# Relative attention with 64-row score products: each half of the matrix array works on its own eight sequences

## The chip, the cores and the metric

The kernel runs on one core of a Trainium2 chip. The metric is the device time of one execution in microseconds (us), as the median of the runs. The profile of one execution gives, for each engine, when every instruction began and how long it took: PE is the matrix engine's products and PEld its loads of stationary operands, DVE the vector engine, ACT the scalar engine, POOL the general engine, SP the engine that issues most transfers.

## The reference

Sixteen sequences of 512 rows by 128 features go through a layer norm, and then through two branches that are added to the input: an attention with relative positions (16 heads of 8 features), and a network of three layers with weights of plus and minus one. Cut to what matters:

```
xn = layernorm(x)                                   # x: 16 x 512 x 128
q, k, v = heads of layernorm2(xn) @ Wq, Wk, Wv (+ biases)     # 16 heads of 8
p = heads of pe @ Wp                                # 512 positions
content = einsum('bihd,bjhd->bhij', q + u_bias, k)
pos     = relative_shift(einsum('bihd,jhd->bhij', q + v_bias, p))
attn    = softmax((content + pos) * scale, axis=-1)
head    = einsum('bhij,bjhd->bihd', attn, v)
out     = x + head @ Wo + bo + ffn(xn)
```

`relative_shift` pads each row of `pos` with a zero and reads the result back in rows of 512, so that query row i and key j meet the position at a distance that depends on j - i; above the diagonal the values are those of query row i + 1.

## The kernel before, in words

**Setup.** Norms, the three layers, and the projections of queries, keys and values come first. Queries and keys are kept as high and low halves of 16 bits, so that a product over 8 features becomes one over 4 parts x 8 = 32 rows. They are stored to scratch in HBM (`qu_scr`, `qv_scr`, `k_scr`, `p_scr`, `pd_scr`) and loaded again head by head. The stores of `qv_scr` are `quads_stored` (lines 595 to 602), eight transfers a call, issued by SP. Two of its four calls stand between the end of the projections and the first scores.

**Units.** Attention works in units: one head and 16 query rows (4 rows in each of 4 blocks of 128), all 16 sequences, all 512 keys. There are 16 heads x 32 = 512 units. The scores of a unit lie with the keys on the partitions, in two PSUM banks of 512 values: bank 0 has key blocks 0 and 1, bank 1 has key blocks 2 and 3, each with all 16 sequences. There are three pairs of such banks (`s_t`, line 791), so that a unit's banks come free when the exponentials of the unit three back have been taken.

**Scores** (`scores`, line 799, called for each half). All products have 128 rows. The stationary operand of a content product (line 811) holds the keys of four sequences, 32 rows each; the moving operand holds the queries of the four sequences beside zeros, so that one product of 64 columns gives the scores of four sequences. A half unit has 8 content products of 64 columns, 4 position products off the diagonal (line 827, two of 128 and two of 64 columns) and 2 on it (line 840, 64 columns).

**Maxima.** DVE takes the maximum over the first bank's two key blocks (`max_first`, L854), then folds in the two blocks of the second bank (`max_second`, L859, twice). PE turns the result with two transposes (L864), and DVE takes the maximum over the keys (L868), negated. PE adds it to the scores with four products of 256 columns (L873, two for each bank), and ACT takes the exponential of each bank (L883), written for the pair of 16 units into a large tile in SBUF, of which there are two.

**Values.** `weighted` (L904) multiplies one sequence group's exponentials with the values and a column of ones: four products with 9 stationary columns each, placed at columns 0, 32, 64 and 96 of the array, in 32-bit precision, which the profile shows as two records each. A pair of 16 units has 16 such blocks; two are issued in each cycle, one behind the other.

**Order.** The order of PE, DVE and ACT is written out by hand: `STEPS` (line 41) lists one cycle, which is two units, and each engine works through its own steps in that order. There are 256 full cycles. A step `A0` belongs to the first unit of the cycle, `G1-` to the second unit of the cycle before. A and B are the two halves of the scores, F, G and H the maxima, T the transposes, N the maximum over keys, X and Y the subtraction and exponential of each half, V two blocks of values. SP issues the loads for the next heads and query rows in between (`load_queries`, `load_head`, two of them at each A step). When a pair is done, its sums go to HBM by POOL's queue, are divided there and come back; the output projection is spread over later cycles (`first_output`, `rest`, `direct`). `direct` (L1066) has products with a 9-row stationary operand at rows 0, 32, 64 and 96.

Of the kernel before, what the change touches and what calls it, by code (L numbers as in the profile page):

```python
# [40 lines left out]
STEPS = "N0- A0 B0 G1- H1- X0- F0 Y0- T1- N1- V G0 X1- A1 Y1- H0 T0 B1 F1"  # L41
# [17 lines left out]
def attention_order():  # L59

    cycles = UP // 2
    last = H * NU // 2
    for c in range(last + 1 + cycles):  # L70
        for step in STEPS.split():
            if step == "V":
                if c > cycles:
                    yield "V", *divmod(c - 1 - cycles, cycles)
                elif c < cycles:
                    yield "W", c
                continue
            late = step.endswith("-")
            if late <= c < last + late:
                yield step[0], 2 * (c - late) + int(step[1])  # L80
# [3 lines left out]
def rel_attention_and_binary_ffn(  # L84
# [53 lines left out]
    qv_scr = scr("qv_scr", [4, DH * H, 5, NL, NC, UL, B], F16)  # L138
# [23 lines left out]
    win = [cst(f"win_{n}", [P, 2, WIN], F16) for n in range(2)]  # L162
    win_d = [cst(f"win_d_{n}", [P, 2, WIND], F16) for n in range(2)]
    q_t = [cst(f"q_{n}", [P, 16, S], F16) for n in range(2)]
    qc_t = [t[:, :4].rearrange("p g (n i m) -> p g n i m", n=2, m=2) for t in q_t]
    qp_t = [t[:, 4:12].rearrange("p (s r) (a u b) -> p s r a u b", s=2, a=NC, u=UL) for t in q_t]
    qd_t = [t[:, 12:].rearrange("p (t r) (a u b) -> p t r a u b", t=2, a=NC, u=UL) for t in q_t]
# [15 lines left out]
    def load_head(h, m):  # L183

        src = p_scr.rearrange("t (d h) s j -> (t d) h s j", h=H)[:, h]
        src_d = pd_scr.rearrange("t (d h) s n j -> (t d) h s n j", h=H)[:, h]

        def load(n):
            rows_n = slice(32 * n, 32 * n + 32)
            nc.sync.dma_start(  # L190
                k_t[m][rows_n], k_scr.rearrange("t (d h) b j -> (t d) h b j", h=H)[:, h, n::4, :]
            )
            nc.sync.dma_start(win[m][rows_n], src[:, :, 3 - n : 3 - n + WIN])
            r, side = n // 2, n % 2
            nc.sync.dma_start(win_d[m][rows_n], src_d[:, side, :, 1 - r : 1 - r + WIND])

        return [lambda n=n: load(n) for n in range(4)]
# [4 lines left out]
    def load_queries(h, l):  # L202

        m = l % 2
        qv = qv_scr.rearrange("t (d h) r l a u b -> (t d) h r l (a u b)", h=H)[:, h, :, l]
        qu = qu_scr.rearrange("t (d h) b n i m -> (t d) h b n (i m)", h=H)[:, h]

        def load(n):
            rows_n = slice(32 * n, 32 * n + 32)
            nc.sync.dma_start(  # L210
                qc_t[m][rows_n, :, n // 2].rearrange("p g i m -> p g (i m)"),
                qu[:, n // 2 :: 2, n % 2, 2 * l * P : 2 * (l + 1) * P],
            )
            nc.sync.dma_start(
                qp_t[m][rows_n, :, n].rearrange("p s a u b -> p s (a u b)"), qv[:, n : n + 2]
            )
            r, side = n // 2, n % 2
            nc.sync.dma_start(
                qd_t[m][rows_n, :, r].rearrange("p t a u b -> p t (a u b)"),
                qv[:, r + side : r + side + 3 : 2],  # L220
            )

        return [lambda n=n: load(n) for n in range(4)]


    with ExitStack() as pre:
# [29 lines left out]
        def load_x(b):  # L256
# [12 lines left out]
        after = [next_place(places, [NL * NC, UL, B]) for _ in range(2)]  # L269
        p_half = [  # L270
            t.rearrange("p x u b -> p (x u b)")[:, : PAD + S + PAD] for t in after
        ]
        qv_all = [next_place(places, [4, NQ, B]) for n in range(2)]
# [11 lines left out]
        for t in after:  # L285
            nc.vector.memset(t.rearrange("p x u b -> p (x u b)").bitcast(F32)[:, : PAD + S // 2], 0.0)
# [220 lines left out]
        def clear_queries(b):  # L507

            nc.gpsimd.memset(q_t[b % 2][:, 2 * (b // 2) : 2 * (b // 2) + 2].bitcast(F32), 0.0)
# [29 lines left out]
        def project_q(b):  # L539
# [10 lines left out]
            for m in range(2):  # L550
# [5 lines left out]
                q_banks.rearrange("p n (q r) -> p r q n", r=4), 1, *[q[:, :, :, b : b + 2] for q in qv_all]  # L556
# [28 lines left out]
        def next_quads():  # L585

            for n in range(2):
                first = qv_all[n][:, 0].rearrange("p (x u) b -> p x u b", u=UL)
                end = NL * NC - NC
                nc.scalar.copy(after[n][:, :, : UL - 1], first[:, :, 1:])  # L590
                nc.scalar.copy(after[n][:, :end, UL - 1], first[:, NC:, 0])
                nc.scalar.copy(after[n][:, end : end + NC - 1, UL - 1], first[:, 1:NC, 0])
                nc.vector.memset(after[n][:, end + NC - 1, UL - 1], 0.0)

        def quads_stored(l):
            for n in range(2):
                src = qv_all[n].rearrange("p r (l q) b -> p r l (q b)", l=NL)[:, :, l]
                last = after[n].rearrange("p (l a) u b -> p l (a u b)", l=NL)[:, l]
                for part in Q_PARTS[n]:
                    dst = qv_scr[part].rearrange("f r l a u b -> f r l (a u b)")[:, :, l]  # L600
                    nc.sync.dma_start(dst[:, :4], src)
                    nc.sync.dma_start(dst[:, 4], last)
# [185 lines left out]
    with ExitStack() as att:  # L788
        ps = att.enter_context(tc.tile_pool(name="ps", bufs=1, space=bass.MemoryType.PSUM))

        s_t = [
            [ps.tile([P, 2, NC, 4, B], F32, tag=f"s_{n}_{m}", name=f"s_{n}_{m}") for m in range(2)]
            for n in range(3)
        ]
        t_t = ps.tile([P, 4, 2, P], BF16, tag="t", name="t_t")
        t_bank = t_t.rearrange("p n f i -> p (n f i)").bitcast(F32).rearrange("p (g i) -> p g i", g=2)
        manual = ExitStack()
        manual.enter_context(tc.manual_schedule(engines=ORDERED))
        def scores(n, half, st):

            side_m, u = st["m"], st["u"]
            sp = st["ps"][half]
            blocks = sp.rearrange("p c a r b -> p (c a) r b")
            kt = k_t[side_m]
            m = (u // UL) % 2
            qc = qc_t[m].rearrange("p g n (a i) m -> p g n a i m", a=NC)
            qp, qd = qp_t[m], qd_t[m]
            ul = u % UL
            for c in (2 * half, 2 * half + 1):
                for g in range(4):  # L810
                    nc.tensor.matmul(  # L811
                        sp[:, c % 2, :, :, 4 * g : 4 * g + 4].rearrange("p a r (n m) -> p n (a r) m", m=2),
                        lhsT=kt[:, g, c * P : (c + 1) * P],
                        rhs=qc[:, g, :, :, 4 * ul : 4 * ul + 4].rearrange("p n a r m -> p n a (r m)"),
                        start=(c % 2 == 0 and g == 0),
                        stop=False,
                        skip_group_check=True,
                    )

            for side, off, dist in ((0, LO_OFF, range(-1, -NC, -1)), (1, UP_OFF, range(1, NC))):  # L820
                for d in dist:
                    cs = [c for c in (2 * half, 2 * half + 1) if 0 <= c - d < NC]
                    if not cs:
                        continue
                    x0 = (cs[0] % 2) * NC + cs[0] - d
                    y0 = off + d * P - 4 * u
                    nc.tensor.matmul(  # L827
                        blocks[:, x0 : x0 + (NC + 1) * (len(cs) - 1) + 1 : NC + 1],
                        lhsT=win[side_m][:, side, y0 : y0 + P],
                        rhs=qp[:, side, :, cs[0] - d : cs[-1] - d + 1, ul, :].rearrange(  # L830
                            "p r a b -> p a r b"
                        ),
                        start=False,
                        stop=False,
                        skip_group_check=True,
                    )

            for t in range(2):
                x0 = 2 * half
                nc.tensor.matmul(  # L840
                    blocks[:, x0 : x0 + NC + 2 : NC + 1, 2 * t : 2 * t + 2],
                    lhsT=win_d[side_m][:, t, UP_OFF - 4 * u : WIND - 4 * u],
                    rhs=qd[:, t, :, 2 * half : 2 * half + 2, ul, :].rearrange("p r a b -> p a r b"),
                    start=False,
                    stop=False,
                    skip_group_check=True,
                )
# [4 lines left out]
        def max_first(n, st):  # L852
            st["max"] = wk.tile([P, 2 * P], BF16, tag="m", name=f"m_{n}", bufs=3)
            nc.vector.tensor_reduce(  # L854
                st["max"], flat(st["ps"][0]).rearrange("p c x -> p x c"), AX.X, ALU.max
            )

        def max_second(n, st, c):
            nc.vector.tensor_tensor(st["max"], flat(st["ps"][1])[:, c], st["max"], ALU.max)  # L859

        def transposed(n, st):
            st["pt"] = t_t[:, 0]
            for f in range(2):
                nc.tensor.transpose(st["pt"][:, f, :], st["max"][:, f * P : (f + 1) * P], ident_b)  # L864
# [388 lines left out]
```

## Time and profile before

| | |
|---|---|
| median of 3 runs | 1325.06 us (1322.6 to 1327.06) |
| span of the profiled execution | 1321.9 us |
| PE busy / PEld busy | 1285.4 us (97%) / 951.5 us (72%) |
| DVE busy | 1097.8 us (83%) |
| ACT busy | 862.5 us (65%) |
| POOL busy | 372.5 us (28%) |
| granted PE clock, mean | 0.995 |
| instructions on PE with a profile record | 23149 products, 23149 loads |
| transfers | 177.93 MB, mean 135 GB/s |

The profiled execution has no time of its own beside its span; the span is 3.2 us below the median of the runs. Products overlap on PE, so the busy share says that PE was never empty, not that it was at its best; the distance between the starts of successive products says what each costs. A wait on an engine that is not the bound costs nothing.

### The profile page before, as it was taken

To read this page: it belongs to the slowest core of one execution; us is meant where nothing else is said; L and a number is where in the kernel's file an instruction comes from. 1 tells how busy PE (TensorE), PEld (TensorE's weight loads), DVE (VectorE), ACT (ScalarE), POOL (GpSimd) and SP (SyncE) were. 2 spreads that over 40 slices of the span, in tenths; PEclk is the share of its full clock that TensorE was granted. 3 is DMA by queue.
4 is the path that set the end of the run, shared out by engine and by line. 5 is a ranking of instruction groups with operands and counts; after the bars stand their busy time and mean duration, and the time that the engine had idled before them with its cause. 6 is when DMAs were issued, how large, how long until landed. Compare 5 with 4: busy or idle time off the path is not lost.

```text
span 1321.9 us, 56006 instructions
## 1 busy us (share of the span) xinstructions
PE 1285.4 (97%) x23149; PEld 951.5 (72%) x23149; DVE 1097.8 (83%) x2709; ACT 862.5 (65%) x1421; POOL 372.5 (28%) x610
## 2 busy tenths in 40 slices
PE   5999999899999999999999999999999999999997
PEld 2555555677777777777777777777777777777774
DVE  8988666788888888888888888888888888888884
ACT  4556666566666666666666666666666666666662
POOL 4644200112223222222222222333333332222202
PEclk9999999999999999999999999999999999999998
DMA  5676548944444444444444444445444445544452
GB/s 138 212 244 230 212 172 312 308 120 108 109 107 106 107 106 106 110 106 107 106 107 107 110 108 111 115 114 127 122 120 120 121 117 127 124 108 108 111 110 71
DMA packets 277283, 177.93 MB, mean 135 GB/s; under 512 B 112974, under 2 KB 265588, under 8 KB 276956
## 3 DMA queue, kind: packets, MB, share of 16 engines
q1 hardware_dynamic: 258644, 156.97, 43.1%
q0 software_dynamic: 17296, 16.86, 5.7%
q8 instruction: 182, 2.98, 1.0%
q14 instruction: 73, 0.60, 0.2%
q10 hardware_dynamic: 1088, 0.52, 0.1%
HBM read 114.00 MB, written 56.78 MB: 129 GB/s over the span
## 4 chain that ended last, share of the span: by engine, by line
PE 84%; DVE 4%; DMA 2%; issue 2%; ACT 2%; SPq 1%; POOL 0%; DVEq 0%; ACTq 0%; POOLq 0%
PE a_t L904 18%; PE s L873 18%; PE s L811 17%; PE s L827 12%; PE p L636 5%; PE s L840 4%; PE t_t L864 4%; PE p L571 1%; PE a_t L678 1%; PE q_banks L542 1%; DVE qu_l L518 1%; ACT k L516 1%; DMA q<-qv_scr 1%; DMA qv_scr<-e 1%; PE s L1050 1%
## 5 line engine op out<-in xcount | busy, mean ns | idle before, releaser
L883 ACT ACTIVATE e<-s,e_scale 128x512 f32<-128x512 f32 x1024 | 672.6, 685 | 309.1 <-PE s L873 309.0
L854 DVE TENSOR_REDUCE m<-s 128x256 bf16<-128x512 f32 x512 | 351.6, 687 | 128.7 <-PE s L840 127.0
L859 DVE TENSOR_TENSOR m<-s,m 128x256 bf16<-128x256 f32 x1024 | 429.6, 420 | 18.1 <-PE s L840 0.3
L811 PE MATMUL s<-q,k 128*128 128x64 f16 x8192 | 406.2, 193 | 2.2 <-DVE e L614 1.4
L873 PE MATMUL s<-ident_b,nm 128*128 128x256 bf16 x2048 | 352.0, 274 | 3.2 <-DVE nm L868 3.2
L827 PE MATMUL s<-q,win 128*128 128x128 f16 (+1 forms) x4096 | 342.1, 206 | 0.3 <-DMA q<-qv_scr 0.3
L811 PEld LDWEIGHTS <-k 128*128 128x128 f16 x8192 | 334.7, 98 | 9.1 <-issue 2.6
L904 PE MATMUL a_t<-e,v 128*9 128x256 f32 x4032 | 266.3, 382 | 1.8 <-issue 1.3
L827 PEld LDWEIGHTS <-win 128*128 128x128 f16 x4096 | 231.6, 98 | 0.5 <-DMA q<-qv_scr 0.4
L873 PEld LDWEIGHTS <-nm 128*128 128x128 bf16 x2048 | 144.8, 98 | 117.5 <-DVE m L859 79.2
L840 PE MATMUL s<-q,win_d 128*128 128x64 f16 x2048 | 227.5, 193 | 0.0
L868 DVE TENSOR_REDUCE nm<-t_t 128x2 bf16<-128x256 bf16 x512 | 209.5, 409 | 4.2 <-PE t_t L864 4.1
L943 POOL DMA_DIRECT2D rden_scr<-den x58 | 32.4, 559 | 476.8 <-DVE nm L868 447.9
L904 PEld LDWEIGHTS a_t<-e,v 128*9 128x9 f32 x4032 | 86.6, 90 | 82.2 <-issue 2.7
L864 PE MATMUL t_t<-ident_b,m 128*128 128x128 bf16 x1024 | 140.8, 219 | 0.5 <-DVE m L859 0.4
L840 PEld LDWEIGHTS <-win_d 128*128 128x128 f16 x2048 | 129.8, 98 | 0.0
L935 POOL DMA_DIRECT2D sum_scr<-av x232 | 117.7, 514 | 0.0
L864 PEld LDWEIGHTS <-m 128*128 128x128 bf16 x1024 | 81.2, 97 | 31.9 <-DVE m L859 1.6
L636 PEld LDWEIGHTS <-e 128*128 128x128 f16 x512 | 49.4, 98 | 58.3 <-issue 10.3
L613 ACT ACTIVATE h2h<-p 128x512 f16<-128x512 f32 x60 | 35.8, 597 | 44.7 <-PE p L636 44.7
L614 DVE SCALAR_TENSOR_TENSOR h2l<-p,h2h 128x512 f16<-128x512 f32 x60 | 41.1, 687 | 28.6 <-ACT h2h L613 28.6
L636 PE MATMUL p<-h1h,e 128*128 128x512 f16 x240 | 62.3, 379 | 0.7 <-DVE h1l L614 0.7
(176 smaller groups left out, 978.7 us busy)
## 6 DMA issues: line engine op xcount, KB each, us to landing
q<-qv_scr SPq DMA_DIRECT2D x512, 64.0 KB, 2.2
q<-qu_scr SPq DMA_DIRECT2D x256, 64.0 KB, 2.7
k<-k_scr SPq DMA_DIRECT2D x128, 128.0 KB, 3.2
win<-p_scr SPq DMA_DIRECT2D x128, 79.5 KB, 3.1
v<-v_scr SPq DMA_DIRECT2D x32, 288.0 KB, 4.7
k_scr<-hv SPq DMA_DIRECT2D x64, 128.0 KB, 2.1
qu_scr<-k SPq DMA_DIRECT2D x16, 512.0 KB, 3.6
qu_scr<-qu_l SPq DMA_DIRECT2D x16, 512.0 KB, 4.8
```

The lines of the kernel that those rows point to most:

```text
L636: nc.tensor.matmul(ph, lhsT=w[:, t, f * P : (f + 1) * P], rhs=h[t][m], start=(m == 0 and t == 0), stop=(m == 1 and t == n - 1),)
L811: nc.tensor.matmul(sp[:, c % 2, :, :, 4 * g : 4 * g + 4].rearrange("p a r (n m) -> p n (a r) m", m=2), lhsT=kt[:, g, c * P : (c + 1) * P], ...
L827: nc.tensor.matmul(blocks[:, x0 : x0 + (NC + 1) * (len(cs) - 1) + 1 : NC + 1], lhsT=win[side_m][:, side, y0 : y0 + P], rhs=qp[:, side, :, ...
L840: nc.tensor.matmul(blocks[:, x0 : x0 + NC + 2 : NC + 1, 2 * t : 2 * t + 2], lhsT=win_d[side_m][:, t, UP_OFF - 4 * u : WIND - 4 * u], rhs=q ...
L854: nc.vector.tensor_reduce(st["max"], flat(st["ps"][0]).rearrange("p c x -> p x c"), AX.X, ALU.max)
L859: nc.vector.tensor_tensor(st["max"], flat(st["ps"][1])[:, c], st["max"], ALU.max)
L864: nc.tensor.transpose(st["pt"][:, f, :], st["max"][:, f * P : (f + 1) * P], ident_b)
L868: nc.vector.tensor_reduce(st["nm"], st["pt"], AX.X, ALU.max, negate=True)
L873: nc.tensor.matmul(flat(st["ps"][half])[:, :, f * P : (f + 1) * P], lhsT=st["nm"][:, f : f + 1].to_broadcast([P, P]), rhs=ident_b.unsqueez ...
L883: nc.scalar.activation(st["eT"][:, :, cs, :, i0 : i0 + 4].rearrange("p b c a r -> p (c a) b r"), st["ps"][half].rearrange("p c a r b -> p ...
L904: nc.tensor.matmul(bank[32 * r : 32 * r + VW, g], lhsT=v_t[pair["m"]][:, v0 : v0 + VW], rhs=pair["eT"][:, b, c], start=(c == 0), stop=(c = ...
L935: queue.dma_start(sum_scr[h, :, b : b + 2, :], av[32 * r : 32 * r + DH])
```

## The change

The scores of a unit are split by sequences and not by keys. Bank 0 has sequences 0 to 7 with all four key blocks, bank 1 has sequences 8 to 15. Every score product has 64 rows, two sequences or two query offsets of 32 rows each: rows 0 to 63 of the array write bank 0, rows 64 to 127 write bank 1, and the two are issued in turn. Each has half the columns or fewer: a unit has 32 content products of 32 columns (line 820 of the changed kernel), 24 position products of 48, 32 or 16 columns (line 845) and 8 of 32 columns on the diagonal (line 858), where it had 16, 8 and 4. The layouts of `qu`, `qv`, `win`, `win_d` and `q_t` follow.

DVE takes the maximum over all four key blocks of a bank in one reduction (line 873), two a unit. The maxima are turned by eight products with 32 stationary columns (line 884), into a 32-bit tile, and no longer by two transposes. The subtraction has four products of 64 rows and 256 columns (line 902). ACT's two exponentials (line 916) have the same number of elements. The values of a cycle are issued as two blocks in two places. `STEPS` is new: K is content, P positions, F the maximum of one bank (F0 and F1 are the banks of the first unit, F2 and F3 those of the second), S the subtraction, E both exponentials, V0 and V1 one block of values each. Two minus signs mean two cycles back, and the values start one cycle later. There is one more tile, `end_res`, for the residual at the end.

```diff
-STEPS = "N0- A0 B0 G1- H1- X0- F0 Y0- T1- N1- V G0 X1- A1 Y1- H0 T0 B1 F1"
+STEPS = "V0 F1- K1- S1-- E1-- P1- T0- N0- F2- F3- V1 S0- E0- K0 P0 F0 T1- N1-"
+BEHIND = 2
...
-    for c in range(last + 1 + cycles):
+    for c in range(last + BEHIND + cycles):
...
-    qv_scr = scr("qv_scr", [4, DH * H, 5, NL, NC, UL, B], F16)
+    qv_scr = scr("qv_scr", [4, DH * H, 2, 5, NL, NC, UL, B // 2], F16)
...
-                qp_t[m][rows_n, :, n].rearrange("p s a u b -> p s (a u b)"), qv[:, n : n + 2]
-            )
...
+            for side in range(2):
+                nc.sync.dma_start(
+                    qp_t[m][rows_n, side, odd::2].rearrange("p r a u b -> p r (a u b)"),
+                    qv[:, half, odd + side : odd + side + 3 : 2],
+                )
...
-                    nc.sync.dma_start(dst[:, :4], src)
-                    nc.sync.dma_start(dst[:, 4], last)
+                    for k in range(2):
+                        nc.sync.dma_start(dst[:, k, :4], src[:, k])
+                    nc.sync.dma_start(dst[:, :, 4], last)
...
+        NB = 6
+        banks = [ps.tile([P, NC, NC, 4, B // 2], F32, tag=f"s_{n}", name=f"s_{n}") for n in range(NB)]
...
+            for c in range(NC):
                 for g in range(4):
+                    for k, sp in enumerate(st["ps"]):
+                        ks = slice(64 * k, 64 * k + 64)
+                        nc.tensor.matmul(
+                            sp[:, c, :, :, 2 * g : 2 * g + 2].rearrange("p a r m -> p (a r) m"),
+                            lhsT=k_t[side_m][ks, g, c * P : (c + 1) * P],
+                            rhs=qc[ks, g, :, 4 * ul : 4 * ul + 4].rearrange("p a r m -> p a (r m)"),
...
+            for two in range(2):
+                rs = slice(2 * two, 2 * two + 2)
+                for side, off, dist in ((0, LO_OFF, range(-1, -NC, -1)), (1, UP_OFF, range(1, NC))):
+                    for d in dist:
+                        cs = [c for c in range(NC) if 0 <= c - d < NC]
...
+                        for ks, blocks in tiles:
+                            nc.tensor.matmul(
...
+        def max_of_keys(n, st, half):
+            if half == 0:
+                st["max"] = wk.tile([P, 2 * P], BF16, tag="m", name=f"m_{n}", bufs=3)
+            nc.vector.tensor_reduce(
+                st["max"][:, half * P : (half + 1) * P],
+                flat(st["ps"][half]).rearrange("p c x -> p x c"),
...
+            for h in range(2):
+                for j in range(4):
+                    x0 = P * (j // 2) + 64 * h + 32 * (j % 2)
                     nc.tensor.matmul(
+                        t_t[32 * j : 32 * j + 32, h],
+                        lhsT=st["max"][:, x0 : x0 + 32],
+                        rhs=ident_b,
...
+            for h in range(2):
+                for k in range(2):
+                    ks = slice(64 * k, 64 * k + 64)
                     nc.tensor.matmul(
+                        flat(st["ps"][k])[:, :, 64 * h : 64 * h + 64],
+                        lhsT=st["nm"][ks, h : h + 1].to_broadcast([64, P]),
+                        rhs=ident_b[ks, ks].unsqueeze(1).to_broadcast([64, NC, 64]),
```

## The prediction, made before the changed kernel had run

> **What bounds the kernel now.** I read the page's engine shares and its chain of waits first.
>
> ```profile
> PE 1285.4 (97%) x23149; PEld 951.5 (72%) x23149; DVE 1097.8 (83%) x2709; ACT 862.5 (65%) x1421; POOL 372.5 (28%) x610
> ...
> PE 84%; DVE 4%; DMA 2%; issue 2%; ACT 2%; SPq 1%; POOL 0%; DVEq 0%; ACTq 0%; POOLq 0%
> ```
>
> 84% of the path that ended last is PE. Next, the timeline of 700 to 705 us, one cycle of two units: start, length, engine, line, operation.
>
> ```profile
> 700.26 0.11 PEld L873 LDWEIGHTS <-nm 128*128 128x128 bf16 x2 [0.43 <-DVE m L859]
> ...
> 700.50 0.40 PE L811 MATMUL s<-q,k 128*128 128x64 f16 x8
> ...
> 701.23 0.69 DVE L854 TENSOR_REDUCE m<-s 128x256 bf16<-128x512 f32 x1 [0.50 <-PE s L840]
> ...
> 701.84 0.41 DVE L868 TENSOR_REDUCE nm<-t_t 128x2 bf16<-128x256 bf16 x1
> ...
> 702.17 0.87 DVE L859 TENSOR_TENSOR m<-s,m 128x256 bf16<-128x256 f32 x2
> ...
> 702.96 0.68 DVE L854 TENSOR_REDUCE m<-s 128x256 bf16<-128x512 f32 x1
> 703.09 1.26 ACT L883 ACTIVATE e<-s,e_scale 128x512 f32<-128x512 f32 x2 [1.03 <-PE s L873]
> 703.09 0.12 PEld L864 LDWEIGHTS <-m 128*128 128x128 bf16 x2
> 703.11 0.28 PE L864 MATMUL t_t<-ident_b,m 128*128 128x128 bf16 x2
> ...
> 703.31 1.05 PE L904 MATMUL a_t<-e,v 128*9 128x256 f32 x16
> ```
>
> Eight content products, each 193 ns by the page's group, span 0.40 us, so they start (400-193)/7 = 29 ns apart; the next step starts 0.23 us after the first. The same reading gives 56 ns for 128 columns (two L864 in 0.28 us, 219 each) and 110 ns for 256 (L873). That is about 0.42 ns a column and 2 ns a product: PE is set by columns streamed, and the loads of 128 columns hide behind 64 columns. The cycle's sum: 4 half-scores of 0.46, 8 subtractions of 0.11, 4 transposes of 0.056, 16 value records in four waves 0.22 apart (0.88), and two changes between full products and 9-column ones. Each change costs 0.09: after the transposes the next product was due at 703.23 and came at 703.31; after the values at 704.20, and came at 704.30. Sum 1.84+0.88+0.22+0.88+0.18 = 4.00. The chain has a values step at 699.35, 703.38 and 707.41: 4.03 a cycle. 256 cycles are 1032 of the 1321.9 us.
>
> DVE is next: its starts lie 0.60 apart after L854, 0.33 after L868, 0.79 for two L859, so 2x(0.60+0.33+0.79) = 3.44 of 4.03.
>
> **The change, part by part.** *Score products.* A unit's 28 products become 64, in 32 pairs (one for rows 0-63, one for rows 64-127), of 16 to 48 columns, mean 32. Two questions decide. Do the two of a pair run side by side? The chain at the end of before has products on four separate row groups, L1066, beside full ones of 128 columns, L1050:
>
> ```profile
> 1305.34 2.44 PE s L1050 x16
> 1307.78 0.74 PE s L1066 x16
> ...
> 1312.52 1.10 PE s L1050 x8
> ```
>
> Sixteen on four row groups take 0.74, sixteen on all rows 2.44 (eight 1.10): row groups do run side by side, loads included. And what does a pair of 32 columns cost? No row has under 64 columns at this pace. From below: two loads of 98 ns span 0.11 and 0.12 us (L873, L864), so a second load follows the first by 12 to 22 ns, 17 in the middle, and a load of 128 columns stands before every product. From above, if side by side: the 29 ns of 64 columns; if not, twice 20 to 29. I take the load's row, since at 32 columns (0.42x32+2 = 15 ns) the load is longer than the stream, plus a few ns for handing from load to product: 20 ns a pair. X, the scores of a unit, is 32x20 = 0.64 us, against 0.92 now. Its ends: 0.54 (17 ns) and 0.93 (29 ns), and 1.28 if the products don't run side by side (64x20).
>
> The Trainium skill, TensorEngine Tiling (Array Packing), Instruction Overhead, speaks against this: it gives each matmul about 60 cycles of overhead and says not to take the tiling factor from a dimension that is already small. At the 2.4 GHz of its page TensorE: Matmul & The Clock Gate that is an estimated 25 ns a pair, X = 0.80, and by the sums below the time would be about 1321 us, too near to 1325 to be told from no change by much; no row here has so short a product to try it on.
>
> *Subtraction.* Four products of 256 columns, in two side-by-side pairs: 2x0.11 = 0.22 a unit, 0.44 before. *Turning.* Eight products of 128 columns on four column groups, as L904 runs its own: two waves of 0.056, as before, 0.28 to the end of the last. *Values.* The same four waves, in two places. *Changes of form:* four a cycle, not two: +0.18. *PE's sum:* 2X + 0.44 + 0.22 + 0.88 + 0.36 = 1.90+2X = 3.18 for X = 0.64. PE is no longer full.
>
> *DVE.* Two reductions a unit, each over one bank of 512 values as L854's now, 0.60 each, and L868's 0.33: 2x(1.20+0.33) = 3.06 a cycle. But F1- and N0- now stand next to each other in STEPS with the turn between them, where before another maximum lay between. DVE waits there: 0.69-0.60 for the end of F1, a hand-over, 0.28, a hand-over. Hand-overs: 0.11 from PE to DVE (L840's end 701.12 to 701.23), 0.04 from PE to ACT (700.66 to 700.70, L873 to L883); towards PE I estimate 0.08, between these. That wait is 0.56, so DVE needs 3.62. *ACT:* two exponentials 1.26 (703.09), 2.52 a cycle, covered.
>
> *The new loops.* With no engine full, the order sets the pace. First, banks: K0 writes the banks that E1-- of the same cycle has read, and both exponentials now wait for all four subtractions. N1 0.41, hand-over 0.08, subtraction to its end 0.11+0.27, to ACT 0.04, two exponentials 1.26, back to PE 0.08, X, the last product's tail 0.17 (0.193 less what X counts), to DVE 0.11, F0 0.60, and N1 again: 3.13+X. Second, PE in its order: N1 0.41+0.08, S1 0.22, P1 0.5X, change 0.09, T0 0.28+0.11, N0 0.41+0.08, S0 0.22, K0 and P0 X, tail 0.17+0.11, F0 0.60: 2.78+1.5X. The second rules above X = 0.70. For 0.64 the loops give 3.77 and 3.74, DVE 3.62, PE 3.18: the cycle is 3.77, and 256x(3.77-4.03) = -67 us.
>
> *SP and the rest.* `quads_stored` has three transfers where it had two: four more a call, two calls on the path at 219-239 us, 0.43 to 1.08 each (L601), and `load_queries` four more of 0.43 behind each: 2x4x0.6+2x4x0.43 = +8, from +3 (halved stores that issue faster) to +13. Behind those SP transfers stand the first scores, so this is paid in full. Later four more loads per eight units are 1.7 us in some 15, on an SP queue that has 12 loads of 0.43 there: hidden. The values start a cycle later: +1 at the end. Clearing half of `q_t` is POOL's, beside the layers. If the wider gap of SP were used up, a late load would show as PE waiting for `q`.
>
> Sum on the profile's own span: 1321.9-67+9 = 1264. The median stood 3.2 above that span: 1267.
>
> **Rivals.** *Pairs at the load's pace* (17 ns, X = 0.54): cycle 3.67, -92+9, time 1242. For it: nothing in the four row groups' 0.74 us shows an extra; against it: that stage has 129 columns, where small costs hide. *A floor per product* (slower): if a short product costs a row group as much as one of 64 columns, 29 ns, X = 0.93, the second loop gives 4.18, +38+9: 1372. It decides from X = 0.81, where 2.78+1.5X plus 9/256 reaches 4.03. For it: no row shows a product at under 28 ns from the one before in the same rows; against it: the 29 ns are explained by the columns. *The products don't run side by side, or PE can't be fed* (slower): 336 instructions a cycle for 168; X = 1.28, the second loop 4.70, +172+9: 1506. For it: even L1066 and L904 average 28 ns or more a product, so no row shows a lasting rate above what before has; against it: the 2.44 to 0.74. Finally, the change could leave the cycle where it is because of the loops alone: with X of 0.80 to 0.82 the time is within 0.3%, about what a measurement of this kernel can tell from no change.
>
> **How the numbers follow.** The forecast, pairs at 18 to 24 ns, X = 0.58 to 0.77: 36%, time 1250 to 1305 of its own. At the load's pace 14%. At the floor, 25 to 30 ns: 30%, 1315 to 1380. Not fed or not side by side: 20%. The range leaves out most of the last: 1238 to 1385. Faster by over 0.3%: the first two, less a little for loops that I undercount, 0.48; within 0.3%, from the low end of the floor case, 0.07; slower 0.45.
>
> **What would show it.** Right: eight or more content products of line 820 starting 10 ns apart on average (20 a pair); L902's products in pairs; DVE idle before L895 released by the turn of L884, some 0.5 us a cycle; PE's busy share falling from 97%, with waits on ACT's e (banks) among its releasers; a cycle of 3.7 to 3.8. Wrong: starts of 13 ns or more on average (25 a pair), PE still on most of the chain, DVE waiting for P. The sum fails if PE waits for `q` loads, or if idle time of PE has no releaser (instructions late).

## The result, and the profile after

The changed kernel takes 1611.69 us (median of 4 runs, 1610.22 to 1613.42) against 1324.99 us (1322.6 to 1327.06) for the kernel before: ratio 1.216, 95% interval 1.2145 to 1.218. The forecast of 1267 us and its whole range, up to 1385, are missed. The profiled execution of after spans 1608.4 us.

The page of after: busy times, then granted clock by slices, the queue that brings instructions, and the chain of waits by engine.

```profile
PE 1319.9 (82%) x44653; PEld 870.5 (54%) x44653; DVE 1041.4 (65%) x2197; ACT 841.2 (52%) x1423; POOL 368.0 (23%) x610
...
PEclk9999999898999999999999999999998999998998
...
q8 instruction: 350, 5.73, 1.6%
...
PE 57%; issue 16%; DVE 8%; ACT 2%; DMA 0%; DVEq 0%; ACTq 0%; SPq 0%
```

No engine is full: PE fell from 97% to 82%, DVE from 83% to 65%. A part that the chain of before had at 2% is now 16%: "issue", time in which PE waited for nothing that the profile shows. The groups by line say where (after the bar: busy us, mean ns of one; then idle us before them, and what ended most of it):

```profile
L895 DVE TENSOR_REDUCE nm<-t_bank 128x2 bf16<-128x256 f32 x512 | 211.9, 414 | 328.3 <-PE t_bank L884 326.9
L820 PEld LDWEIGHTS <-k 64*128 64x128 f16 x16384 | 272.9, 94 | 195.4 <-issue 184.6
...
L845 PE MATMUL s<-q,win 64*128 64x32 f16 (+2 forms) x12288 | 278.7, 175 | 84.0 <-issue 83.0
...
L858 PE MATMUL s<-q,win_d 64*128 64x32 f16 x4096 | 214.5, 174 | 27.2 <-issue 27.2
L884 PE MATMUL t_bank<-ident_b,m 128*32 128x128 bf16 x4096 | 169.7, 234 | 28.6 <-issue 26.7
```

DVE's wait for the turn (L895) comes once a cycle, as predicted: behind F1- it is 1.2 us on average, for the other unit almost nothing (328.3 us over 256 cycles is 1.28 us, where 0.56 was forecast). But nearly every large group of PE has idle time without a releaser, which the page calls "issue". One such stall in PE's timeline:

```profile
904.43 0.30 PE L845 MATMUL s<-q,win 64*128 64x48 f16 x12
904.59 0.18 PE L858 MATMUL s<-q,win_d 64*128 64x32 f16 x2
905.63 0.19 PE L858 MATMUL s<-q,win_d 64*128 64x32 f16 x2 [0.87 <-issue]
905.67 0.29 PE L845 MATMUL s<-q,win 64*128 64x48 f16 x12
```

In the middle of four products that need nothing new, PE stands still for 0.87 us. Two counts on the trace's own starts explain it. Number all that the trace has of PE in order of start (loads, products and the 257 other entries of its sequencer), and count the numbers in rounds of 256. In the middle stage (400 us from the start to 250 us before the end) number 193 comes 244 times, and 212 times it starts more than 0.15 us after the one before it; no other number does so more than 11 times. And q8 moved 350 packets of 16 KB, while 2x44653 records / 256 = 349; before, 182 packets for 2x23149/256 = 181. So a packet is a page of 256 PE instructions, and number 193 is where a page ends. (The page of a run still means its profile.) Around this stall, a packet runs from 902.99 to 904.33, PE goes on at 905.63, and the next packet starts at 906.89: 1.34 to fetch, 1.30 until PE runs it, 1.26 until the next fetch begins, 3.90 in all. Over all pages with a stall at both ends, 181 of them, these are 1.15, 1.41 and 1.39 us on average, and the page interval is 3.94 us (standard deviation 0.36). In before pages are 6.16 us apart, and a page's packet has ended 4.5 us before PE reaches the page.

A cycle of before has 168 records, one of after 336. At 3.94 us for 256, 336 take 5.17 us; measured over 150 cycles (the distance of the reductions that give the negated maximum, L895, before L868), after takes 5.21 us a cycle and before 4.08. The difference, 1.12 us x 256 = 287 us, is the whole of the 286.7 us lost.

### The profile page after: what moved, and what is told of

It reads as the page before. It is cut to its first block, busy times and chain, and to the rows that moved or that the text cites. A ratio compares the mean times of both kernels' runs of the same rounds, so it can differ in the third digit from the quotient of the medians.

```text
span 1608.4 us, 98587 instructions
## 1 busy us (share of the span) xinstructions
PE 1319.9 (82%) x44653; PEld 870.5 (54%) x44653; DVE 1041.4 (65%) x2197; ACT 841.2 (52%) x1423; POOL 368.0 (23%) x610
## 4 chain that ended last, share of the span: by engine, by line
PE 57%; issue 16%; DVE 8%; ACT 2%; DMA 0%; DVEq 0%; ACTq 0%; SPq 0%
PE s L820 13%; PE s L902 11%; PE a_t L937 10%; PE s L845 9%; PE t_bank L884 8%; DVE nm L895 6%; PE s L858 4%; ACT e L916 1%; PE a_t L1026 1%; DVE m L873 1%; DVE den L972 1%; PE s L1082 1%; ACT part L1040 0%; PE s L1098 0%; PE t_bank L937 0%
## 5 line engine op out<-in xcount | busy, mean ns | idle before, releaser
L916 ACT ACTIVATE e<-s,e_scale 128x512 f32<-128x512 f32 x1024 | 647.6, 683 | 565.7 <-PE s L902 559.8
L873 DVE TENSOR_REDUCE m<-s 128x128 bf16<-128x512 f32 x1024 | 677.8, 683 | 165.5 <-ACT e L916 131.2
L895 DVE TENSOR_REDUCE nm<-t_bank 128x2 bf16<-128x256 f32 x512 | 211.9, 414 | 328.3 <-PE t_bank L884 326.9
L820 PEld LDWEIGHTS <-k 64*128 64x128 f16 x16384 | 272.9, 94 | 195.4 <-issue 184.6
L820 PE MATMUL s<-q,k 64*128 64x32 f16 x16384 | 309.7, 175 | 54.4 <-issue 51.7
L845 PE MATMUL s<-q,win 64*128 64x32 f16 (+2 forms) x12288 | 278.7, 175 | 84.0 <-issue 83.0
L845 PEld LDWEIGHTS <-win 64*128 64x128 f16 x12288 | 250.7, 94 | 101.7 <-issue 94.4
L902 PE MATMUL s<-ident_b,nm 64*128 64x256 bf16 x2048 | 213.9, 285 | 35.8 <-DVE nm L895 5.2
L858 PE MATMUL s<-q,win_d 64*128 64x32 f16 x4096 | 214.5, 174 | 27.2 <-issue 27.2
L884 PE MATMUL t_bank<-ident_b,m 128*32 128x128 bf16 x4096 | 169.7, 234 | 28.6 <-issue 26.7
L902 PEld LDWEIGHTS <-nm 64*128 64x128 bf16 x2048 | 61.4, 95 | 184.8 <-DVE nm L895 158.2
L858 PEld LDWEIGHTS <-win_d 64*128 64x128 f16 x4096 | 132.5, 94 | 29.6 <-issue 29.6
```

The lines of the kernel that those rows point to most:

```text
L820: nc.tensor.matmul(sp[:, c, :, :, 2 * g : 2 * g + 2].rearrange("p a r m -> p (a r) m"), lhsT=k_t[side_m][ks, g, c * P : (c + 1) * P], rhs= ...
L845: nc.tensor.matmul(blocks[:, x0 : x0 + (NC + 1) * (len(cs) - 1) + 1 : NC + 1, rs], lhsT=win[side_m][ks, side, y0 : y0 + P], rhs=qp_t[m][ks ...
L858: nc.tensor.matmul(blocks[:, :: NC + 1, r], lhsT=win_d[side_m][ks, two, y0 : y0 + P], rhs=qd_t[m][ks, r, :, ul, :], start=False, stop=Fals ...
L873: nc.vector.tensor_reduce(st["max"][:, half * P : (half + 1) * P], flat(st["ps"][half]).rearrange("p c x -> p x c"), AX.X, ALU.max,)
L884: nc.tensor.matmul(t_t[32 * j : 32 * j + 32, h], lhsT=st["max"][:, x0 : x0 + 32], rhs=ident_b, start=True, stop=True, skip_group_check=True,)
L895: nc.vector.tensor_reduce(st["nm"], t_t, AX.X, ALU.max, negate=True)
```

## The experiments

Theory "feed": PE gets no more than one page of 256 instructions (loads and products counted together) in some 3.9 us, however little the instructions do. Rival "products": the time is what the products take on the array, plus waits between engines. All cycles below are means over 150 cycles; a run of the kernel before beside each group gave 1325 to 1327 us.

**More array work, the same instructions.** The four subtraction products of a unit, 512 columns wide (the new columns add zeros; `ident_z` is a second identity tile between zeros, made at the start):

```diff
-  flat(st["ps"][k])[:, :, 64 * h : 64 * h + 64],
+  flat(st["ps"][k]),
   lhsT=st["nm"][ks, h : h + 1].to_broadcast([64, P]),
-  rhs=ident_b[ks, ks].unsqueeze(1).to_broadcast([64, NC, 64]),
+  rhs=ident_z[ks, 64 - 64 * h : 192 - 64 * h].unsqueeze(1).to_broadcast([64, NC, P]),
```

> The changed kernel with its four subtraction products written 512 columns wide in place of 256 (the added columns of the moving operand are zeros, so the result is the same). The number of instructions is unchanged; the array gets about 0.11 us a product pair more, 4 pairs a cycle, 0.44 us a cycle, 256 cycles: 113 us. Theory 'feed' (PE gets its instructions one page of 256 at a time, about 3.85 us a page, and 336 instructions a cycle need 5.05 us): most of the added work falls into time in which PE waited for instructions, so 1612 to 1645 us. Rival 'products' (the cycle is the sum of what the products take on the array and of the waits between engines): about 1611 + 113 = 1724 us.

Measured 1577.91 us (1574.5 to 1579.09), ratio to before 1.1889 (1.185 to 1.1928). The added work is there: in the trace a pair of these products costs 0.226 us, not 0.120, which is 109 us over the kernel. Nothing of it appears in the time, so the rival falls. But the time went down by 34 us, below the range of "feed" too; no theory had expected that (see below).

**The kernel before, with more instructions and hardly any work.** Behind each block of value products:

```diff
+            if not at_end:
+                for x in range(42):
+                    nc.tensor.matmul(
+                        a_t[32 * (x % 4) : 32 * (x % 4) + 1, g, :2],
+                        lhsT=zeros_b[:, :1],
+                        rhs=zeros_b,
+                        start=False,
+                        stop=(c == NC - 1),
+                        skip_group_check=True,
+                    )
```

> The kernel before with 42 tiny products added behind each block of value products (one column of zeros as weights, two moving columns, added into the sums of values: the result is the same). 168 + 168 = 336 instructions a cycle, as many as the changed kernel has, and almost no array work: four column quarters can run side by side, 84 products a cycle at about 6 ns each make 0.5 us. Theory 'feed': 336 instructions need 5.05 us, so the cycle goes from 4.03 to about 5.05 and the time to 1325 + 256 x 1.02 = 1586 us (1540 to 1630), with idle time of PE that begins at every 256th instruction. Rival 'products': 4.03 + 0.5 = 4.53 us, 1453 us, with no such idle time.

> As the kernel with 42 tiny products, with 63: 168 + 252 = 420 instructions a cycle. Theory 'feed': 420 / 256 x 3.85 = 6.3 us a cycle, 1325 + 256 x 2.28 = 1909 us (1840 to 1960). Rival 'products': 42 more products a cycle at 6 ns, 0.25 us over the run with 42: about 1517 us.

Measured 1589.92 and 1922.39 us (one run each): 4 and 13 us from what "feed" gives, 137 and 405 from the rival. The tiny products themselves can be read in the timeline of the run with 63:

```profile
602.20 0.66 PE L916 MATMUL a_t<-zeros_b 128*1 128x2 bf16 x63
...
604.76 0.37 PE L813 MATMUL s<-q,k 128*128 128x64 f16 x7
605.73 0.20 PE L813 MATMUL s<-q,k 128*128 128x64 f16 x1 [0.61 <-issue]
```

63 of them span 0.66 us, the last lasting 0.16, so they start 8 ns apart, and 126 cost 1.0 us a cycle, a little more than the 6 ns assumed. A load and a product in 8 ns also say that PE takes the instructions of a page that is there at some 4 ns each: the 15 ns an instruction that a page comes to is not a pace of single instructions. With that the rival would say 4.08 + 1.0 = 5.1 us a cycle; measured is 6.47 us, and the stall stands between two products of a content group that the kernel before runs without one. Its page, L916 first:

```profile
L916 PEld LDWEIGHTS <-zeros_b 128*1 128x1 bf16 x31248 | 345.2, 81 | 231.7 <-issue 140.3
L813 PE MATMUL s<-q,k 128*128 128x64 f16 x8192 | 445.2, 200 | 57.5 <-issue 48.4
```

215 of 324 page ends stall, again at number 193 of 256. So the slowdown of after is made in the kernel before by instructions alone. Nor is it the granted clock, which is lower in after (0.946): with 42 tiny products it is 0.989, before has 0.995, and the time is still 1590 us.

**Fewer instructions in the changed kernel.** Three edits: the eight 32-column turning products as two of 128 (the maxima are written in the order that this needs); the `two = 1` position products left out; all position products left out.

```diff
-            for h in range(2):
-                for j in range(4):
-                    x0 = P * (j // 2) + 64 * h + 32 * (j % 2)
                     nc.tensor.matmul(
-                        t_t[32 * j : 32 * j + 32, h],
-                        lhsT=st["max"][:, x0 : x0 + 32],
+                        t_t[:, h],
+                        lhsT=st["max"][:, h * P : (h + 1) * P],
...
```

```diff
-            for two in range(2):
+            for two in range(1):
```

```diff
-                positions_of(units[n])
```

> The changed kernel with the maxima turned by two products of 128 columns a unit in place of eight of 32 (the maxima are written in the order that this needs; the result is the same): 312 instructions a cycle in place of 336. Theory 'feed': 24 / 256 x 3.9 = 0.37 us less a cycle, 1612 - 94 = 1518 us (1500 to 1540). Rival 'products': two products of 128 columns take 56 ns each, eight of 32 columns side by side in two groups of four about as much, and the changes of tile form stay: 1600 to 1615 us.

> The changed kernel with the position products of two of a quad's four queries left out (16 pairs a cycle of 64; that part of the scores is missing): 272 instructions a cycle. Theory 'feed': 272 / 256 x 3.9 = 4.14 us a cycle, or a little more where other waits take its place: 300 + 257 x 4.14 = 1364 us (1345 to 1390). Rival 'products' at the 25 ns a pair that the trace shows, with no limit from the feed: the sum of the cycle falls by 0.40 us only, 1612 - 103 = 1509 us.

> The changed kernel without its 64 position products a cycle's unit pair (32 pairs a cycle; the position part of the scores is left out, all else stays). 208 instructions a cycle in place of 336. Theory 'feed': 208 instructions need 3.13 us, less than the other loops, so the stalls that begin at every 256th instruction go and VectorE's loop sets the cycle at 3.6 to 3.8 us: 300 + 256 x 3.7 = 1247 us (1220 to 1275). Rival 'products' with 49 ns a pair (what the cycle of 5.05 us would make of 64 pairs): 5.05 - 32 x 0.049 = 3.48 us, also under VectorE's loop, about 1230 us, but with PE's idle time put down to VectorE and none to the issue of instructions in either case; this run only bounds what the rest of the cycle takes.

Measured 1537.22 (1534.98 to 1539.46), 1415.03 (1414.79 to 1415.28) and 1276.36 us (one run). The direction and order are those of "feed"; of its ranges the first is met, half of the positions lies 25 us above its own. The turn in two products saved 74 us where "feed" gave 94 and the rival at most 12. Half of the positions saved 197 us where "feed" gave 248 and the rival 103: 12 ns for each instruction taken out, in both runs, not 15. The page interval is not a constant: it is 3.99 us with 312 instructions a cycle and 4.11 with 272, not 3.94, and over 312 and 272 pages these 0.05 and 0.17 us are 16 and 46 us, most of the 20 and 51 that are missing. With 272 instructions 132 of 185 page ends still stall. The 103 pages with a stall at both ends take 4.15 us: the packet (1.18) and the time until PE goes on (1.41) are as in after, the wait for the next packet is longer (1.57, in after 1.39), and most so where PE takes long over the page's first instructions (correlation 0.73 with the time of the first 64). What starts a packet the record does not show. So the gain fades before the feed ends to bind. The table shows how:

| run | instructions a cycle | us a cycle | us for 256 (middle stage) | page ends with a stall |
|---|---|---|---|---|
| before | 168 | 4.08 | 6.16 | 4 of 109 |
| no positions | 208 | 3.92 | 4.78 | 8 of 131 |
| half of the positions | 272 | 4.42 | 4.11 | 132 of 185 |
| turn in two products | 312 | 4.89 | 3.99 | 181 of 222 |
| after | 336 | 5.21 | 3.94 | 212 of 244 |
| before + 2x42 | 336 | 5.11 | 3.87 | 112 of 243 |
| before + 2x63 | 420 | 6.47 | 3.93 | 215 of 324 |

The run without positions lies 1 us above its range. Its stages in the windows view (busy us of each engine, granted clock, share of DMA, GB/s):

```profile
300.00:500.00 200.00, 188.67 (x5789) 102.01 (x5782) 178.30 (x349) 145.64 (x252) 60.64 (x107) 1.00 0.49 119
900.00:1100.00 200.00, 162.12 (x4725) 87.78 (x4722) 146.44 (x283) 120.31 (x213) 56.08 (x96) 0.91 0.46 113
```

The first has 11571 records, 208 a cycle, so 3.60 us a cycle, where the prediction's VectorE loop says 3.62; the second 9447, so 4.40. In the second PE waits for queries, nine times and 26 us in all; over the whole run it is 41 us:

```profile
L820 PE MATMUL s<-q,k 64*128 64x32 f16 x16384 | 327.4, 174 | 56.1 <-DMA q<-qu_scr 41.2
```

At that pace the loads were no longer hidden, as they are at 5.2 us a cycle; whether SP's longer list or the transfers themselves made them late, no run separates.

**Does the page time depend on the kernel's own transfers?** After, without its loads beyond the first 32 units:

```diff
+                if n >= 2 * UP:
+                    loading.clear()
                 for _ in range(min(2, len(loading))):
                     loading.pop(0)()
```

> The changed kernel without its loads of queries, keys, windows and values after the first 32 of 512 units (later units work on stale data; all else stays). In the trace of after, 181 of 243 pages of 256 PE instructions lie between two stalls, 3.94 us apart: packet 1.14, packet end to PE going on 1.40, to the next packet 1.37 us. Theory 'feed, latency of its own': the page interval does not depend on the kernel's own transfers, 1612 us within 15. Theory 'feed, slowed by transfers': packet and waits shrink, for instance to 3.5 us a page: 1612 - 243 x 0.44 = 1505 us. Rival 'products or loads': if late loads held PE, the stalls at every 256th instruction would be fewer and the time lower by what they held.

Measured 1544.21 us (1543.28 to 1545.14). One stage of after and one of this run, in the transfer view of 700 to 800 us (packets, MB, share of 16 engines):

```profile
q1 hardware_dynamic: 17698, 7.47, 30.2%
q0 software_dynamic: 1423, 1.34, 6.2%
q8 instruction: 25, 0.41, 1.8%
```

```profile
q0 software_dynamic: 1629, 1.54, 7.7%
q8 instruction: 27, 0.44, 1.9%
```

27 pages in place of 25 in the same 100 us. The page interval between stalls is 3.74 us (standard deviation 0.20) in place of 3.94 (0.36); it is the wait for the next packet that shrank (1.39 to 1.21), the packet (1.13) and the time until PE goes on (1.40) hardly. So the loads add 0.2 us a page. 256 cycles of 336 instructions are 336 pages, which makes 67 us, all that the run gained (67 us). The greater part of the interval, 3.7 us, is there without them.

**Why did the wide subtraction make it faster?** Half of the width; the first operand's new place alone; and wide without loads:

```diff
-  flat(st["ps"][k]),
+  flat(st["ps"][k])[:, :, 64 * h :],
-  rhs=ident_z[ks, 64 - 64 * h : 192 - 64 * h].unsqueeze(1).to_broadcast([64, NC, P]),
+  rhs=ident_z[ks, 64 : 192 - 64 * h].unsqueeze(1).to_broadcast([64, NC, P - 64 * h]),
```

```diff
-  rhs=ident_b[ks, ks].unsqueeze(1).to_broadcast([64, NC, 64]),
+  rhs=ident_z[ks, 64:128].unsqueeze(1).to_broadcast([64, NC, 64]),
```

> The changed kernel with two of the four subtraction products of a unit 512 columns wide (those of the first half of the columns), the other two as they were: half of the array work that the run 'wide_subtraction' added, 0.22 us a cycle, the same number of instructions. Theory 'feed': hidden again, 1577 to 1615 us; if more array work as such makes the pages come sooner, about 1595 us. Rival 'products': 1612 + 57 = 1669 us.

> The changed kernel with all four subtraction products 256 columns wide as in the changed kernel, but with their moving operand read from the second identity tile that the runs with wide products built (its making stays in the program). Full and half width gave 1578 and 1576 us, the changed kernel 1612. If the width is what helps (the wide first pair, or the higher granted clock that goes with more array work), this run is back at 1612 us (1605 to 1616). If something that all three edits share, and not the array work, brings the pages sooner (another place of the operand, another alignment of the program), it is at 1575 to 1585 us. Theory 'feed' holds either way: the instructions are the same in number.

> The run 'wide_subtraction' without the loads of queries, keys, windows and values after the first 32 units (stale data). The wide subtraction took 34 us from the changed kernel, the missing loads 68 us. If the wide products helped because the instruction pages met less of the kernel's own transfers, the help is gone here: 1535 to 1555 us, as 'quiet'. If they helped in another way, both add up: about 1510 us.

Measured 1576.21 (1575.71 to 1579.0), 1605.24 (1594.05 to 1613.56) and 1525.91 us (1523.12 to 1528.71). The place of the operand explains little (6 us between the medians, inside the scatter of its runs), and the gain does not grow with the width. Where the subtraction is narrow the mean granted clock is 0.946 (after) and 0.938 (narrow, new place), where it is wide 0.985 and 0.978, and the page intervals go with it: 3.94 and 3.91, then 3.81 and 3.84. Without loads 18 us of the 34 remain, between the two answers expected. The trace says how much of it the clock can be. In the middle stage of after the granted clock is at half in 27 stretches, 99 us together; with the wide subtraction in 2, 7 us together. The 44 pages of after that such a stretch touches take 4.15 us on average, the other 199 take 3.89: some 11 us, of the 29 us that 243 pages of 3.94 in place of 3.82 come to. But pages at full clock are shorter too, 3.89 and 3.81. So the clock is about a third of the gain, and why the rest came, and why the clock was granted, stays open.

**A version of the two parts that need few instructions.** A product's form is the number of rows and columns of the array that it uses (128x128, 64x128, 128x32). Scores stay on 128 rows; only the banks by eight sequences, the maxima bank by bank and the subtraction by row halves are taken over:

```diff
-STEPS = "N0- A0 B0 G1- H1- X0- F0 Y0- T1- N1- V G0 X1- A1 Y1- H0 T0 B1 F1"
+STEPS = "N0- A0 B0 G1- S0- E0- F0 T1- N1- V G0 S1- E1- A1 T0 B1 F1"
...
-            for c in (2 * half, 2 * half + 1):
-                for g in range(4):
+            for c in range(NC):
+                for g in (2 * half, 2 * half + 1):
```

> The kernel before with two parts of the change only: each PSUM bank holds eight sequences (score products keep 128 rows, 32 a unit in place of 28 with fewer columns each), the maximum is taken bank by bank in two passes, and the subtraction is done by two row halves side by side, each in its own bank (four products of 64 rows in place of four of 128). 184 instructions a cycle in place of 168, far under what a page of 256 in 3.9 us lets through. Worked out from the rows: subtraction 0.44 us to 0.24 a unit, position products 0.46 to 0.50, changes of form +0.18 to +0.36 a cycle. Theory 'the row-halved subtraction pays, the 64-row scores do not': cycle 3.85 to 3.98, 1280 to 1312 us. Rival 'the changes of form and VectorE's loop take it back': 1320 to 1345 us.

Measured 1323.82 us (1321.11 to 1328.68, 10 runs), ratio 0.9969 (0.9946 to 0.9992): my theory's range is missed, the rival's met. Its timeline shows the reason:

```profile
500.05 0.22 PE L839 MATMUL s<-q,win_d 128*128 128x64 f16 x2
500.10 0.40 PE L813 MATMUL s<-q,k 128*128 128x64 f16 x8
...
500.53 0.22 PE L839 MATMUL s<-q,win_d 128*128 128x64 f16 x2
500.68 0.39 PE L881 MATMUL s<-ident_b,nm 64*128 64x256 bf16 x4
501.01 0.29 PE L863 MATMUL t_bank<-ident_b,m 128*128 128x128 bf16 x2
501.22 1.05 PE L916 MATMUL a_t<-e,v 128*9 128x256 f32 x16
...
504.69 0.39 PE L881 MATMUL s<-ident_b,nm 64*128 64x256 bf16 x4
```

After two L839 the next product starts 0.05 us later if it has the same form, 0.15 if it is the row-halved subtraction; the two turning products before the 9-column values take 0.21, not 0.11. A change of form costs 0.09 to 0.10 us, and there are five a cycle in place of two. By the distances between starts, summed over 200 units, a cycle saves 0.23 us on subtractions (0.44 to 0.33 a unit, with the change behind them); position products of 32 columns cost 27 ns, nearly what 64 cost, and give back 0.11; the change ahead of the first subtraction gives back 0.09. That leaves 0.02, as measured (4.08 to 4.07). From L881 to L881 two units on it is 4.01 us: PE is full, as before.

**One change of form less.** The turn that stands before the values takes their form:

```diff
+                for j in range(4) if n % 2 else (slice(0, P),):
+                    js = slice(32 * j, 32 * j + 32) if n % 2 else j
                     nc.tensor.matmul(
-                        t_t[:, h],
-                        lhsT=st["max"][:, h * P : (h + 1) * P],
+                        t_t[js, h],
+                        lhsT=st["max"][:, h * P : (h + 1) * P][:, js],
...
```

> The kernel of the run 'both' with the maxima of each odd unit turned by eight products of 32 columns, as the changed kernel does, so that this turning has the tile form of the value products that follow it: one change of form less a cycle, 196 instructions a cycle. In 'both' the last product before a change of form keeps PE about 94 ns longer (123 to 29 ns, 149 to 55 ns) and five changes fall into its cycle of 4.01 us. Theory 'PE is full and each change of form costs it 0.09 us': 4.01 - 0.09 = 3.92 us, 1324 - 23 = 1301 us (1293 to 1310). Rival 'another loop holds the cycle, or the eight products cost what the change saves': 1318 to 1330 us.

Measured 1301.88 us (1295.7 to 1303.22), ratio 0.9803 (0.9775 to 0.9831): 24 us faster than the 1326.13 us of before beside it, as worked out, and the fastest kernel of this study that leaves nothing out.

```profile
500.44 0.39 PE L883 MATMUL s<-ident_b,nm 64*128 64x256 bf16 x4
...
503.25 0.29 PE L865 MATMUL t_bank<-ident_b,m 128*32 128x128 bf16 x8
503.38 1.03 PE L918 MATMUL a_t<-e,v 128*9 128x256 f32 x16
504.34 0.39 PE L883 MATMUL s<-ident_b,nm 64*128 64x256 bf16 x4
```

From the turn to the values it is now 0.13 us, not 0.21, and the cycle from L883 to L883 is 3.90 (4.01 in the run above). Its 12 further instructions (196 a cycle) cost nothing, since 4 of 126 page ends stall.

## Why the prediction was wrong, step by step

*What bounds before.* Held: PE is full, at 4.0 to 4.1 us a cycle.

*Do the two of a pair run side by side?* Yes. In after the second of a pair starts 4 ns after the first, the next pair 21 ns after that (medians).

*What does a pair cost?* Here a term was mis-sized: 20 ns forecast, 25 measured. The distance from one pair to the next within a group is 25 ns for the 32 columns of L820 and L858 and the 16 to 48 of L845 alike, from the 10th to the 75th percentile, so X is 0.80, not 0.64. The Trainium skill's 60 cycles for each matmul, which the prediction weighed (TensorEngine Tiling (Array Packing), Instruction Overhead), come to an estimated 25 ns, and the trace agrees. By the prediction's own loops X = 0.80 gives 3.98 us a cycle and about no change: it takes away the forecast gain and explains none of the 287 us lost. With half of that X (the run without positions, X = 0.40) the first stage had 3.60 us a cycle for the 3.62 that the sum of DVE gives. That agreement is in part luck: DVE was busy 3.21 us of this cycle and waited 0.39 for the turn, where the sum had 3.06 and 0.56. The other two loops were longer than DVE's in the forecast and bound in no run, so they stay untested.

*Subtraction, turning, changes of form, DVE's wait.* Pairs of L902 take 0.117 to 0.120 for 0.11, changes of form 0.09 to 0.10 for 0.09, L895's wait is there, once a cycle, and longer while PE is stalled. SP's +8 us came to 1: the first L895 starts at 244 us, the first L868 of before at 242.

*The step that failed.* "With no engine full, the order sets the pace": the sum had engines and loops, and no term for the supply of instructions. It doubled the records of a cycle from 168 to 336 and charged each only for the array. The missing term is 336/256 x 3.94 = 5.17 us, more than any loop. Its last sign of being wrong, idle time of PE without a releaser, is what came. The last rival named it ("PE can't be fed: 336 instructions a cycle for 168") but put its price down by the other half of its sentence, products one after another with X = 1.28, and so at 1506 us; what ruled was the page, not X. Its argument, that no row has a lasting rate above before's, was the right one and deserved more than 20%, and a price of its own.

*What the page of before could have told.* It has q8 with 182 packets for 46298 records, so the page of 256 was to be seen, and the trace shows one packet a page, 0.5 us behind the page's end on average, and no two under way. Its shortest page interval, 5.44 us, was PE's own pace, so the floor itself was not to be read from before. But 5.44 was all that the row had shown: 336/256 x 5.44 = 7.1 us a cycle was the upper end of this term, and it was left out of the range.

The Trainium skill has the parts of this: Runtime: NRT & Kernel Launch, Instruction fetch mechanics, says that instructions come in blocks of 16 KiB, 256 of them, with the next block fetched while one runs, and that this is mostly hidden. The blocks agree with q8's packets. That it is hidden agrees with the 6.2 us a page of before, and not with after, whose pages hold less than 3.9 us of work.

## What to carry to other kernels

Before splitting products into more and smaller ones, count loads and products together over a cycle: here PE got 256 in 3.7 to 4.1 us where pages stalled, so a stretch of several pages that averages under some 15 ns an instruction is set by their number, whatever they do; idle time of PE with no releaser that begins at every 256th record shows it. Inside a page that is there, a pair of products of 16 to 48 columns on half of the rows each still costs 25 ns, near the 29 of a product of 64 columns on all rows, so narrow products gain little by splitting. Wide ones do: the 256-column subtraction went from 0.44 to 0.24 us a unit, changes of form not counted. What such a split wins can be lost again to changes of form at 0.09 us each, so stages of one form belong next to each other.

## What was not expected of the hardware

- The instruction fetch as a bound: 1.1 us a packet, 1.4 until PE runs it, 1.2 to 1.4 until the next packet starts, one page ahead and not more (in before the next packet waits for the page's end, with 4.5 us to spare); the kernel's own loads lengthen it by 0.2 us a page.
- 109 us of added array work went with a kernel 34 us faster and a granted clock up from 0.946 to 0.985; half of that work did the same. About a third of it is the clock, the rest is open.
- With pauses of some 0.8 us in each page, the granted clock of after is 0.92 to 0.96 over stages of 200 us of the attention part, where before has 1.00. It comes from stretches at half clock; in the middle stage they cost some 11 of 958 us. No run sets the pauses apart from the clock, so what lowers it is not shown.
